# A decoder layer (gated scan, cross-attention, feed-forward) in fp32: first transfers in another order, padded weights fetched in whole rows, and a second table of places for units 0, 1 and 15

## The chip, the cores and the metric

One core of a Trainium2 chip runs the kernel. The metric is the device time of one execution in microseconds (us); host work (laying arrays out) is not in it. The five engines are named as in the profile: PE (TensorE; PEld is its weight load), DVE (VectorE), ACT (ScalarE), POOL (GpSimd) and SP (SyncE, which here only issues transfers). ACT issues transfers too.

## The reference

All in float32, with B = 4 sequences of 1024 tokens, width 256, 16 heads of 16 channels.

```python
# 1. a state-space layer (Mamba-2 form), per head h, state size 64
logA = x_h @ W_logA + b_logA
X, Bm, Cm = split(silu(x_h @ W_XBC + b_XBC))        # 16, 64, 64 channels
cum  = cumsum(logA over time)
Y    = (exp(cum_i - cum_j) for j <= i) * (Cm @ Bm.T) @ X
x    = layernorm(x + ((x_h @ W_gate + b_gate) * Y) @ W_out.T + b_out)
# 2. cross-attention to 77 context tokens per sequence, with a mask
q = x @ q_w + q_b ; k, v = split(ctx @ kv_w + kv_b)
x = layernorm(x + softmax(q k.T / 4, masked) v @ proj_w + proj_b)
# 3. feed-forward, 256 -> 1024 -> 256, ReLU
x = layernorm(x + relu(x @ W1 + b1) @ W2 + b2)
```

## The kernel before

The 4096 tokens are cut into 16 **units** of 256 tokens, four to a sequence; a unit has two chunks of 128. Each unit u passes three stages: A (state-space layer, `stage_a` and `chunk_a`), B (attention, `stage_b`) and C (feed-forward, `stage_c`). The scan over 1024 tokens is done chunk by chunk: inside a chunk by a masked 128x128 matrix per head, between chunks through a 64-wide state.

Every small piece of a stage is a **part** with a name and a place. `WHEN` (L36) gives each name a number, and unit u's part stands at u + WHEN[name]; all parts of all units, and the setup blocks (names with s_), are sorted by that number and emitted in that order (L1069). Each engine runs its instructions in the order in which they were emitted, so the table sets the order of the work on all five engines and on the two transfer queues. A place of -1.9 means: about two units ahead of the unit's own time.

The pieces that the change and the prediction touch:

- `load_u(u)` (L142) fetches xu, the unit's input with the features on the partitions: 256 KB in 256 rows of 1 KB, and the source is walked as `a x k t` with a of size 2 outermost. Two of its readers are pl (L486, the logA projection, on PE) and px (L618).
- `load_t(u)` (L150) fetches the same input in another layout (xt, four transfers of 16 partitions) for pb (L556), the projection to Bm and Cm.
- pl goes to cum (L494, a scan on DVE), cum to DRAM (cd, L501), and from there cd is read back broadcast to all partitions: four transfers dl (L509, 512 KB each, one per chunk c and half k, dl00 to dl11) and ec (L516). The exponentials on ACT (ex, L679), the causal select on POOL (sel, L687) and the product with pg on DVE (st, L711) work on dl in place. de (L651, DVE) reads a corner of dl.
- bct (L576, DVE) with th (L568, ACT) is the silu of pb; pg (L701), ptb (L719), pc (L752), py (L798), pyo (L737), poa (L825) are stage A's other matmuls. pq (L855), pm (L880), pe (L927), pa (L952) and pob (L988) are stage B's, ph (L1018) and pf (L1045) are stage C's. pk (L363) and pv (L394) make the keys and values once.
- The setup blocks fetch constants: s_x (L176) the first xu and xt, w_bc, w_l, b_l; s_g the weights w_x, b_x, w_g on ACT's queue; s_x2 scales w_x and b_x by 0.5 on POOL (L236); s_c the context, the weights of keys and values, k_b and the masks; s_o the gate's bias b_g in eight transfers (L303) and w_out in eight (L310); s_q the queries' weights; s_p, s_1, s_2 the later weights. `packed` (L260) fetches the keys' or queries' weights, which lie padded in DRAM (16 used columns of each 32), in pieces of 16 columns.

Transfers from SP and ACT share eight completion semaphores. A transfer that is given a semaphore again waits, in its queue, until the former transfer with that semaphore has landed; all that stands behind it in that queue waits too.

Of the kernel before, what the change touches and what calls it, by code (L numbers as in the profile page):

```python
# [18 lines left out]
S = 77  # L19
FF = 1024  # L20
P = 128
# [12 lines left out]


WHEN = {  # L36
    "s_c": -11.4319, "s_z": -9.9133, "s_x": -9.8561, "load_u1": -8.0656, "s_g": -6.4870,
    "keys": -5.3615, "s_l": -4.6719, "s_x2": -4.4990, "values1": -4.1376, "s_bc": -3.7603,
    "values3": -3.4250, "load_u": -2.5586, "values2": -1.9971, "pl": -1.8803, "cum": -1.8531,
    "keys0": -1.8267, "px1": -1.7594, "zx1": -1.7162, "px0": -1.5890, "cd": -1.5818,  # L40
    "load_t": -1.5536, "zx0": -1.5509, "pcum": -1.4767, "ncum": -1.4509, "s_p": -1.2104,
    "thx0": -1.1705, "thx1": -1.1208, "dl00": -1.0934, "dl01": -1.0768, "dl10": -0.9492,
    "dl11": -0.9057, "keys1": -0.8509, "s_o": -0.8374, "de0": -0.8294, "pb0": -0.8117,
    "th00": -0.8019, "xz1": -0.7953, "ex00": -0.7869, "bct00": -0.7866, "th01": -0.7453,
    "bct01": -0.6793, "sel00": -0.6211, "xz0": -0.6048, "load_k0": -0.5874, "pb1": -0.5858,
    "ec": -0.5819, "ex01": -0.5770, "sel01": -0.5599, "ptb00": -0.5404, "th10": -0.5257,
    "bct10": -0.5205, "pgt": -0.5199, "bk00": -0.4948, "gT": -0.4894, "dex0": -0.4785,
    "xw0": -0.4447, "th11": -0.4309, "de1": -0.4269, "bct11": -0.4250, "pg00": -0.3724,
    "pg01": -0.3720, "st00": -0.3610, "st01": -0.3602, "ex11": -0.3481, "sel11": -0.3410,
    "ptb01": -0.3408, "bk01": -0.2802, "ex10": -0.2757, "ecx": -0.2676, "pyo0": -0.2315,  # L50
    "pc0": -0.2303, "py0": -0.2272, "pg11": -0.2257, "pg10": -0.2148, "ptb10": -0.1983,
    "load_k": -0.1849, "xb": -0.1554, "ya0": -0.1481, "yg0": -0.1318, "bk10": -0.0982,
    "sn0": -0.0665, "pts0": -0.0616, "sel10": -0.0538, "st11": -0.0434, "dex1": -0.0212,
    "new0": -0.0173, "xw1": -0.0163, "st10": 0.0043, "ptb11": 0.0094, "poa0": 0.0190,
    "s_q": 0.0209, "bk11": 0.0220, "pyo1": 0.0432, "r10": 0.0459, "py1": 0.0504, "mv_a0": 0.0672,
    "rs_a0": 0.1161, "ya1": 0.1433, "pc1": 0.1487, "ln_a0": 0.1570, "sn1": 0.1632, "yg1": 0.1757,
    "poa1": 0.2004, "pts1": 0.2036, "r11": 0.2185, "mv_a1": 0.2296, "values0": 0.2451,
    "new1": 0.2563, "rs_a1": 0.3220, "ln_a1": 0.3476, "pt_b0": 0.4352, "pt_b1": 0.4430,
    "xT_b": 0.4675, "pq": 0.5617, "q": 0.5703, "pm1": 0.7199, "mx1": 0.7334, "pm0": 0.7620,
    "mx0": 0.7696, "pmt": 0.9324, "qm0": 0.9930, "qm1": 0.9996, "pe0": 1.0418, "es00": 1.0464,  # L60
    "s_2": 1.0775, "pe1": 1.0783, "es01": 1.0868, "pa0": 1.1557, "es10": 1.1603, "es11": 1.1757,
    "ot0": 1.1769, "om0": 1.1956, "pa1": 1.2797, "x1b": 1.2868, "ot1": 1.2885, "om1": 1.3653,
    "o1": 1.4120, "o0": 1.4426, "pob0": 1.4994, "pob1": 1.5308, "r20": 1.5433, "mv_b0": 1.5643,
    "r21": 1.5897, "rs_b0": 1.5947, "mv_b1": 1.6135, "rs_b1": 1.6195, "ln_b0": 1.6688,
    "ln_b1": 1.7529, "pt_c1": 1.8663, "pt_c0": 1.9377, "s_1": 2.0149, "xT_c": 2.0215,
    "x2b": 2.0830, "ph0": 2.1982, "ph1": 2.3198, "h0": 2.3291, "h1": 2.3786, "ph2": 2.4035,
    "ph3": 2.4579, "h2": 2.4605, "h3": 2.5019, "pf00": 2.6426, "pf01": 2.7349, "r30": 2.7932,
    "pf10": 2.8269, "mv_c0": 2.9076, "pf11": 3.0362, "r31": 3.0394, "mv_c1": 3.1693,
    "rs_c0": 3.6344, "ln_c0": 3.9014, "rs_c1": 3.9589, "out0": 3.9632, "ln_c1": 4.0359,
    "out1": 5.0081,  # L70
}


# [1 line left out]
def decoder_layer_kernel(ctx: ExitStack, tc: tile.TileContext, a: dict, out: bass.AP):  # L75
# [27 lines left out]

    def part(u, name):
        def put(fn):
            jobs.append((u + WHEN[name], len(jobs), name, fn))

        return put

# [37 lines left out]
        )  # L147
        xus[u] = xu

    def load_t(u):  # L150
        for r in range(4):
            nc.sync.dma_start(
                out=xts[u % 2][32 * r : 32 * r + CH],
                in_=a["xT"][CH * r : CH * r + CH, :, u * T : (u + 1) * T],
            )
# [19 lines left out]

    @setup("s_x")  # L176
    def _():
        load_u(0)
        nc.vector.memset(w_l0, 0.0)
        nc.vector.memset(w_l, 0.0)  # L180
        nc.vector.memset(b_l, 0.0)
        for half in range(2):
            rows_ = slice(64 * half, 64 * half + 64)
            nc.scalar.dma_start(out=w_l0[rows_, half], in_=xgl[0:64, half, :, 128:XW])
        for k in range(2):
            nc.scalar.dma_start(
                out=b_l[32 * k : 32 * k + 8],
                in_=xgl[64:65, :, k, 128:XW].rearrange("o a r -> r a o"),
            )
        nc.vector.memset(xts[0], 1.0)  # L190
        load_t(0)
        nc.vector.memset(w_bc, 0.0)
        for r in range(4):
            own = slice(NS * (r % 2), NS * (r % 2) + NS)
            nc.scalar.dma_start(
                out=w_bc[32 * r : 32 * r + CH],
                in_=a["w_bc"][CH * r : CH * r + CH, :, :, r // 2, own],
            )
        nc.scalar.dma_start(
            out=w_bc[CH::32], in_=a["w_bc"][64].rearrange("g b q (n s) -> (q n) (g b) s", n=2)  # L200
        )
        make_identity(nc, ident)
        nc.gpsimd.tensor_copy(b_l[64:128], b_l[0:64])

# [11 lines left out]

    @setup("s_g")
    def _():
        nc.gpsimd.memset(w_x, 0.0)
        nc.gpsimd.memset(w_g, 0.0)  # L220
        for half in range(2):
            rows_ = slice(64 * half, 64 * half + 64)
            nc.scalar.dma_start(
                out=b_x[:, half], in_=xgl[64, half, :, 0:64].partition_broadcast(P)
            )
            nc.scalar.dma_start(out=w_x[rows_, :, half, :], in_=xgl[0:64, half, :, 0:64])
            for k in range(2):
                nc.scalar.dma_start(
                    out=w_g[rows_, k, :, half, :],
                    in_=xgl[0:64, half, k, 64:128].rearrange("x (r c) -> x r c", c=CH),  # L230
                )
# [25 lines left out]

    ctx_ = {}

    def packed(n, kk):  # L260

        return a[n][kk * P : kk * P + P].rearrange("p g (r c) -> p (g r) c", c=32)[:, :, 0:CH]

    def by_heads(t, n):

# [6 lines left out]
    @setup("s_c")  # L272
    def _():
        kv_w = tile_([P, FF // P, T], "hT", "kv_w", bufs=1)
        ctx_.update(k_w=kv_w[:, 0:2], v_w=kv_w[:, 4:6])
        for n, f in (("valid", 2), ("kc", 6)):
            ctx_[n] = kv_w[:, f : f + 2].rearrange("p f t -> p (f t)")[:, 0 : B * S].rearrange(
                "p (b s) -> p b s", b=B
            )
        ctxT = ctx_["ctxT"] = tile_([P, 2, 2 * T], "qm", "ctxT", bufs=1)  # L280
        v_b = ctx_["v_b"] = tile_([S, D], "on", "v_b", bufs=2)
        nc.sync.dma_start(
            out=ctxT[:, :, 0 : B * S], in_=a["ctxT"].rearrange("(k p) s -> p k s", p=P)
        )
        nc.sync.dma_start(out=ctx_["v_w"], in_=a["v_w"].rearrange("(k p) e -> p k e", p=P))
        for kk in range(2):
            nc.sync.dma_start(
                out=ctx_["k_w"][:, kk].rearrange("p (m c) -> p m c", c=CH), in_=packed("k_w", kk)
            )
        nc.sync.dma_start(out=v_b, in_=a["v_b"].partition_broadcast(S))  # L290
        by_heads(k_b, "k_b")
        nc.sync.dma_start(
            out=mrow.rearrange("p b s -> p (b s)"), in_=a["mask"][0].partition_broadcast(P)
        )
        nc.sync.dma_start(out=mcol, in_=a["maskT"])
        nc.gpsimd.memset(vz, 1.0)

    @setup("s_o")
    def _():
        for half in range(2):  # L300
            for r in range(4):
                at = 32 * r + CH * half
                nc.sync.dma_start(  # L303
                    out=b_g[at : at + CH],
                    in_=xgl[64, half, :, 64 + CH * r : 64 + CH * r + CH].rearrange("k c -> c k"),
                )
        for half in range(2):
            for r in range(4):
                at = 32 * r + CH * half
# [5 lines left out]

    @setup("s_q")
    def _():
        for kk in range(2):
            nc.sync.dma_start(
                out=q_w[:, kk].rearrange("p (m c) -> p m c", c=CH), in_=packed("q_w", kk)  # L320
            )
        by_heads(q_b, "q_b")

    @setup("s_p")
# [825 lines left out]
```

## Time and profile before

| | |
|---|---|
| median of 3 runs | 717.74 us (717.26 to 718.21) |
| the profiled execution | 715.87 us, of which the span from first to last instruction is 714.2 us |
| PE busy | 678.8 us, 95% of the span |
| DVE, ACT, POOL busy | 546.9, 413.9, 275.6 us |
| first matmul that reads xu (L486) | 19.77 us into the span |
| first dl transfer issued (L509) | 30.43 us |
| first matmul of unit 0 for Bm and Cm (L556) | 34.77 us |
| PE in each 100 us between 200 and 600 us | busy 100.00 us |
| TensorE clock granted, mean of the span | 0.972 of full |

The profile is one execution; its times are about 1.9 us under the median of the runs. "Busy" of PE counts a matmul from its start to its modelled end, so a busy PE may still run at half clock; the clock row must be read beside it. A row of the timeline begins with its start and its length, then engine, line and what is written and read, and in brackets the idle time before it and what ended that.

### The profile page before, as it was taken

What the parts mean: (1) busy time and instruction counts of PE and PEld (TensorE: products, weight loads), DVE (VectorE), ACT (ScalarE), POOL (GpSimd) and SP (SyncE); (2) the same over time, 40 slices, a digit from 0 to 9 for tenths busy, and PEclk for the clock granted to TensorE, in tenths of its full rate; (3) what the DMA queues carried; (4) which work ended last, traced back from release to release, by engine and by line L of the source; (5) the groups of instructions that cost most, each with busy time, mean ns of one, the idle gap of its engine ahead of it and who ended that gap; (6) DMA issues with size and microseconds to landing.
All of it is one profiled execution on the core that took longest, in us unless ns stands there. A gap on an engine that the chain in (4) does not pass through costs nothing.

```text
span 714.2 us, 19432 instructions
## 1 busy us (share of the span) xinstructions
PE 678.8 (95%) x7744; PEld 538.8 (75%) x7744; DVE 546.9 (77%) x1337; ACT 413.9 (58%) x1091; POOL 275.6 (39%) x441
## 2 busy tenths in 40 slices
PE   2588999999999999999999999999999999999996
PEld 1256767887878787787878788787878788787785
DVE  2376899878888787888788887888878788877652
ACT  0185787747585665748576474847566474843210
POOL 3133355334433443343433434353434334342241
PEclk8578999999999999999999999999999999999999
DMA  5456755224240423424140422424042332200001
GB/s 89 93 144 144 185 173 165 78 61 122 68 116 18 127 61 96 103 75 123 53 124 24 123 76 75 123 61 128 25 123 62 101 83 75 61 17 1 16 16 37
DMA packets 104566, 61.47 MB, mean 86 GB/s; under 512 B 15695, under 2 KB 102172, under 8 KB 104476
## 3 DMA queue, kind: packets, MB, share of 16 engines
q1 hardware_dynamic: 101632, 59.83, 31.9%
q8 instruction: 61, 1.00, 0.5%
q10 hardware_dynamic: 2844, 0.41, 0.4%
q14 instruction: 29, 0.24, 0.1%
HBM read 54.98 MB, written 5.24 MB: 84 GB/s over the span
## 4 chain that ended last, share of the span: by engine, by line
PE 87%; DMA 6%; ACT 2%; SPq 2%; DVE 1%; issue 1%; POOL 0%; POOLq 0%; ACTq 0%; DVEq 0%
PE pf L1045 16%; PE ph L1018 16%; PE pg L701 8%; PE pb L556 5%; PE pe L927 5%; PE pa L952 4%; PE po_b L988 4%; PE py L798 4%; PE pq L855 4%; PE po_a L825 4%; DMA xu<-in_xT_dram 3%; PE ptb L719 3%; PE pm L880 3%; PE py L737 2%; PE pc L752 2%; PE pgt L585 2%
## 5 line engine op out<-in xcount | busy, mean ns | idle before, releaser
L679 ACT ACTIVATE dl<-dl,ncum 128x128 f32<-128x128 f32 x512 | 156.3, 395 | 1.7 <-DVE de L651 1.7
L1045 PE MATMUL pf<-w,hT 128*128 128x256 f32 x512 | 123.5, 386 | 0.0
L1018 PE MATMUL ph<-T_c,w 128*128 128x256 f32 x512 | 121.0, 385 | 0.0
L1018 PEld LDWEIGHTS ph<-T_c,w 128*128 128x128 f32 x512 | 93.7, 190 | 23.0 <-issue 5.9
L938 ACT ACTIVATE es<-pe,mb 77x512 f32<-77x512 f32 x128 | 76.9, 679 | 52.4 <-PE pe L927 51.3
L1045 PEld LDWEIGHTS pf<-w,hT 128*128 128x128 f32 x512 | 93.8, 190 | 15.5 <-issue 2.4
L687 POOL TENSOR_SCALAR_AFFINE_SELECT dl<-dl 128x1024 f32<-128x1024 f32 x64 | 70.0, 1094 | 48.0 <-ACT dl L679 48.0
L711 DVE TENSOR_TENSOR dl<-pg,dl 128x512 f32<-128x512 f32 x128 | 80.7, 683 | 6.4 <-PE pg L701 5.5
L576 DVE SCALAR_TENSOR_TENSOR bct<-th,pb 128x512 f32<-128x512 f32 x128 | 80.9, 673 | 4.3 <-ACT th L568 4.0
L568 ACT ACTIVATE th<-pb 128x512 f32<-128x512 f32 x128 | 69.1, 594 | 22.4 <-PE pb L556 22.2
L726 ACT COPY bk<-ptb 128x512 f32<-128x512 f32 x56 | 32.8, 585 | 75.8 <-PE ptb L719 75.5
L701 PE MATMUL pg<-bct 64*128 64x128 f32 x1024 | 67.3, 279 | 1.2 <-DVE bct L576 1.0
L701 PEld LDWEIGHTS pg<-bct 64*128 64x128 f32 x1024 | 60.4, 188 | 10.7 <-DVE bct L576 6.0
L891 DVE TENSOR_REDUCE maxes<-pm 128x4 f32<-128x308 f32 x128 | 52.2, 471 | 19.9 <-PE pm L880 19.9
L666 POOL TENSOR_TENSOR xw<-xz,de 128x128 f32<-128x128 f32 x56 | 21.3, 402 | 81.7 <-ACT de L658 80.5
L819 POOL TENSOR_TENSOR yg<-ya,gT 128x256 f32<-128x256 f32 x28 | 21.4, 766 | 68.6 <-DVE ya L812 54.2
L556 PE MATMUL pb<-xt,w_bc 17*64 17x256 f32 x1024 | 44.0, 408 | 2.1 <-DVE bct L576 2.1
L440 POOL TENSOR_SCALAR rs_a<-mv_a 128x1 f32<-128x1 f32 x32 | 7.1, 222 | 94.4 <-DVE mv_a L435 94.4
L1034 ACT ACTIVATE hT<-ph,b 128x256 f32<-128x256 f32 x64 | 26.8, 470 | 27.1 <-PE ph L1018 24.7
L970 POOL TENSOR_TENSOR on<-at,rec 128x256 f32<-128x256 f32 x32 | 21.5, 673 | 54.0 <-DVE rec L965 53.3
L787 ACT COPY state<-pts 64x128 f32<-64x128 f32 x56 | 14.5, 258 | 44.3 <-PE pts L777 44.0
L913 DVE SCALAR_TENSOR_TENSOR qm<-q,own,pmt 128x512 f32<-128x512 f32 x32 | 22.5, 744 | 18.4 <-PE pmt L904 18.4
(122 smaller groups left out, 1247.6 us busy)
## 6 DMA issues: line engine op xcount, KB each, us to landing
dl<-cd SPq DMA_DIRECT2D x64, 512.0 KB
xu<-in_xT_dram SPq DMA_DIRECT2D x16, 256.0 KB
xt<-in_xT_dram SPq DMA_DIRECT2D x64, 64.0 KB
xk<-in_x_dram SPq DMA_DIRECT2D x16, 256.0 KB
ec<-cd SPq DMA_DIRECT2D x16, 256.0 KB
out_dram<-r SPq DMA_DIRECT2D x32, 128.0 KB
w<-in_w_dram SPq DMA_DIRECT2D x2, 1024.0 KB
cd<-cum SPq DMA_DIRECT2D x16, 64.0 KB
```

Of the source, the lines that this page charges most:

```text
L556: nc.tensor.matmul(pbs[r][64 * half : 64 * half + 64, bc, :], lhsT=w_bc[rs, 2 * gk + half, bc, :], rhs=xt[rs, 2 * gk + half, :], start=Tru ...
L568: nc.scalar.activation(th, s[f"pb{gk}"][r], AF.Tanh)
L576: nc.vector.scalar_tensor_tensor(t, s[f"th{gk}{r}"], 1.0, s[f"pb{gk}"][r], ALU.add, ALU.mult)
L679: nc.scalar.activation(dl[:, h, :], dl[:, h, :], AF.Exp, bias=s["ncum"][:, 2 * c + k, h : h + 1],)
L687: nc.gpsimd.affine_select(out=dl, in_=dl, compare_op=ALU.is_ge, fill=0.0, base=0, pattern=[[0, 8], [1, P]], channel_multiplier=-1,)
L701: nc.tensor.matmul(pgs[half][:, r, :], lhsT=t[lo : lo + 64, 0, cs], rhs=t[lo : lo + 64, 1, cs], start=True, stop=True,)
L711: nc.vector.tensor_tensor(d, v[f"pg{k}"][half], d, ALU.mult)
L891: nc.vector.tensor_reduce(mx[:, :, at : at + 2], s[f"pm{c}"][r].rearrange("p k a s -> p a k s"), AX.X, ALU.max, negate=True,)
L927: nc.tensor.matmul(pes[r][:, par, :], lhsT=kT[rs, gp, par, bs], rhs=s["qm"][rs, par, gp, :], start=True, stop=True,)
L938: nc.scalar.activation(e, s[f"pe{gp}"][r], AF.Exp, bias=mb[:, b : b + 1], scale=CH**-0.5)
L1018: nc.tensor.matmul(ph[:, j, :], lhsT=w1[:, k, f * P : (f + 1) * P], rhs=s["xT"][:, k, :], start=(k == 0), stop=(k == 1),)
L1045: nc.tensor.matmul(pf, lhsT=s["hT"][:, f, c * P : (c + 1) * P], rhs=w2[:, f, :], start=(f == 0), stop=(f == FF // P - 1),)
```

## The change

1. In s_x the first transfers are issued in the order xt and w_bc alternating, then xu, then w_l and b_l; before it was xu, w_l, b_l, xt, w_bc. The memsets of w_x and w_g move from s_g to s_x.
2. `packed` fetches the padded rows whole (2 KB runs), into a scratch part of the kv_w tile, and two POOL copies take the used columns out. It serves the keys' and the queries' weights. The tiles `valid` and `kc`, which lay in kv_w, get two buffers of the unitT ring.
3. The eight b_g transfers become a block of their own, s_b, ahead of s_o.
4. All numbers of `WHEN` are new, and `EDGE` gives units 0, 1 and 15 places of their own, which `part` prefers. The setup blocks move in `WHEN`: s_x stands first now, s_c after s_g and s_x2; s_p goes from -1.2 to 1.1, s_q from 0.0 to 0.4, s_2 from 1.1 to 1.7 and s_1 from 2.0 to 1.5.

The order that results on SP's queue is: xt x4, xu(0), cd(0), ctxT, v_w, k_w, v_b, k_b x2, two masks, dl00, dl01, xu(1), ec, b_g x8, dl10, dl11, xk, w_out x8, b_out, cd(1), xk(1), xt(1) x4, dl01(1), ec(1), xu(2), dl00(1), dl10(1), cd(2), q_w, q_b x2, dl11(1). On ACT's queue: w_bc x5, w_l x2, b_l x2, b_x, w_x, w_g x2, b_x, w_x, w_g x2, and then the first computing instruction. PE begins with pl, pb, pgt, pcum, px of unit 0 and no longer with pv.

```diff
 WHEN = {
-    "s_c": -11.4319, "s_z": -9.9133, "s_x": -9.8561, "load_u1": -8.0656, "s_g": -6.4870,
...
-    "load_t": -1.5536, "zx0": -1.5509, "pcum": -1.4767, "ncum": -1.4509, "s_p": -1.2104,
...
+    "s_x": -9.0759, "s_l": -6.2209, "s_g": -6.2074, "s_bc": -5.0504, "s_x2": -4.4536,
+    "s_c": -3.7665, "load_u1": -3.4533, "s_z": -2.9306, "s_b": -2.5309, "load_u": -2.2285,
+    "pl": -1.9502, "cum": -1.9128, "load_k0": -1.9113, "s_o": -1.7308, "px1": -1.7147,
...
+EDGE = {
+    0: {
+        "pl": -4.8683, "pb0": -4.8549, "th00": -4.7365, "pgt": -4.7343, "cum": -4.5273,
...
+        "ec": -3.3456, "de0": -3.2299, "bct11": -3.1934, "ex00": -3.1334, "dex0": -2.9623,
+        "ex01": -2.9401, "xz0": -2.7667, "sel00": -2.6907, "dl10": -2.4731, "ptb01": -2.4202,
...
+    1: {
+        "px0": -3.0462, "zx0": -2.7658, "pl": -2.6367, "cum": -2.4709, "cd": -2.4365,
+        "pcum": -2.3348, "load_k": -2.1146, "load_t": -1.9876, "px1": -1.9399, "zx1": -1.7487,
...
+    15: {
+        "load_u": -4.4549, "load_k": -2.9211, "pl": -2.1881, "cum": -2.0838, "px1": -2.0769,
...
     def part(u, name):
         def put(fn):
-            jobs.append((u + WHEN[name], len(jobs), name, fn))
+            place = EDGE.get(u, {}).get(name, WHEN[name])
+            jobs.append((u + place, len(jobs), name, fn))
...
     @setup("s_x")
     def _():
+        nc.vector.memset(xts[0], 1.0)
+        nc.vector.memset(w_bc, 0.0)
+        for r in range(4):
+            load_t(0, [r])
+            own = slice(NS * (r % 2), NS * (r % 2) + NS)
+            nc.scalar.dma_start(
+                out=w_bc[32 * r : 32 * r + CH],
+                in_=a["w_bc"][CH * r : CH * r + CH, :, :, r // 2, own],
+            )
+        nc.scalar.dma_start(
+            out=w_bc[CH::32], in_=a["w_bc"][64].rearrange("g b q (n s) -> (q n) (g b) s", n=2)
+        )
         load_u(0)
...
-    def packed(n, kk):
-
-        return a[n][kk * P : kk * P + P].rearrange("p g (r c) -> p (g r) c", c=32)[:, :, 0:CH]
+    def packed(t, n):
+        pad = ctx_["kv_w"][:, 0:4].rearrange("p (k f) t -> p k (f t)", k=2)
+        nc.sync.dma_start(out=pad, in_=a[n].rearrange("(k p) g m -> p k (g m)", p=P))
+        for kk in range(2):
+            nc.gpsimd.tensor_copy(
+                t[:, kk].rearrange("p (m c) -> p m c", c=CH),
+                pad[:, kk].rearrange("p (m c) -> p m c", c=32)[:, :, 0:CH],
+            )
...
-    @setup("s_o")
+    @setup("s_b")
     def _():
         for half in range(2):
             for r in range(4):
...
     @setup("s_q")
     def _():
-        for kk in range(2):
-            nc.sync.dma_start(
-                out=q_w[:, kk].rearrange("p (m c) -> p m c", c=CH), in_=packed("q_w", kk)
-            )
+        packed(q_w, "q_w")
         by_heads(q_b, "q_b")
```

## The prediction

> **What bounds the kernel now.** I read first the page's busy times and slices, then the stretches of the span, then the chain that ended last and the timeline around its pieces.
>
> ```profile
> PE 678.8 (95%) x7744; PEld 538.8 (75%) x7744; DVE 546.9 (77%) x1337; ACT 413.9 (58%) x1091; POOL 275.6 (39%) x441
> PE   2588999999999999999999999999999999999996
> PEclk8578999999999999999999999999999999999999
> ```
>
> PE is full from the fourth slice (of 17.9 us) to the last but one. What can be won lies at both ends, or in the order in which PE runs the same matmuls.
>
> ```profile
> 10.00:20.00 10.00, 0.23 (x6) 0.23 (x8) 2.85 (x11) 0.00 (x0) 0.00 (x0) 0.61 0.25 63
> 20.00:30.00 10.00, 3.17 (x14) 1.56 (x7) 4.12 (x12) 1.80 (x2) 1.37 (x2) 0.50 0.42 90
> 40.00:50.00 10.00, 8.99 (x73) 6.17 (x73) 7.11 (x17) 10.00 (x31) 2.94 (x4) 0.68 0.39 98
> 60.00:70.00 10.00, 9.97 (x108) 6.93 (x108) 6.42 (x19) 6.42 (x20) 1.86 (x3) 0.66 0.73 138
> 200.00:300.00 100.00, 100.00 (x1182) 80.00 (x1175) 82.69 (x201) 66.26 (x174) 40.47 (x62) 1.00 0.35 93
> ```
>
> Columns: stretch, its length, PE, PEld, DVE, ACT, POOL busy, granted clock, DMA share, GB/s. Between 10 and 20 us PE waits while the DMA engines are a quarter busy; at 60 to 70 the clock is 0.66. Priced at the pace of the middle (each matmul at its mean start-to-start step between 120 and 640 us), PE's work sums to 659 us. So 55 us are lost: 39 by 60.03 us, 10 more by 110, nothing from there to 660, 1 to 700, and 5 after the last matmul.
>
> ```profile
> 8.17 11.47 DMA xu<-in_xT_dram
> 22.21 8.20 DMA cd<-cum
> 33.66 8.19 DMA dl<-cd
> 48.38 11.52 DMA xu<-in_xT_dram
> ```
>
> The start is a chain of transfers; each row is start and length. xu(0) releases pl at 19.77 us, cd and dl bring the first decay matrices at about 39, and xu(2) ends PE's last long wait:
>
> ```profile
> 60.03 0.66 PE L486 MATMUL pl<-xu,w_l 128*32 128x128 f32 x8 [2.15 <-DMA xu<-in_xT_dram]
> 63.98 0.17 DVE L651 TENSOR_TENSOR de<-dl,ncum 128x8 f32<-128x8 f32 x1 [1.54 <-DMA dl<-cd]
> 74.86 0.17 DVE L651 TENSOR_TENSOR de<-dl,ncum 128x8 f32<-128x8 f32 x1 [1.90 <-DMA dl<-cd]
> 674.95 2.66 PE L952 MATMUL pa<-es,vz 77*32 77x256 f32 x16
> 679.47 1.07 PE L952 MATMUL pa<-es,vz 77*32 77x256 f32 x16
> ```
>
> **The change, part by part: the start.** I follow the new queues.
>
> First, xu(0). The xt memset (0.91 us, from 0.87) releases SP at 1.8; four xt issues at 0.64 each, xu at 4.7. What does xu take? It took 11.5 us twice, and from 14 to 19.6 us, with little but xu moving, the trace gives
>
> ```profile
> DMA packets 336, 0.26 MB, mean 46 GB/s; under 512 B 106, under 2 KB 336, under 8 KB 336
> ```
>
> At 46 GB/s its 256 KB last 5.7 us. The Trainium skill (DMA: Bandwidth & Descriptors, "Why a DMA increments its semaphore by 16 and not by 1") says why: a transfer uses as many engines, up to 16, as divide the slowest dimension of both views, and xu's source has a 2 outermost. Two engines at the page's 27 GiB/s would be an estimated 4.5 us. Three xu transfers stand in the chain below; by the rule's figure the result would be 3.6 us earlier. The row decides. I allow 8.6 us from issue to landing (about 1 to start, 5.7, and 2 for what shares its engines): xu(0) at 13.3, 6.4 us before now.
>
> Next, dl00. ACT's w_g gets xu(0)'s semaphore, so six loads of ACT go out from 13.4 at 0.63 us each, to 17.4. The table load (1.28) and the first tanh stand behind them, 18.7, still ahead of any now. dl00 gets the last w_g's semaphore: landed about 19.3, dl00 issued at 19.7 against 30.43. On SP before it stand cd (after pl and cum, 14.6), ctxT, v_w, k_w, v_b, k_b, masks; at about 0.5 us each they pass by then. dl00 and dl01 land by 27 (four took 8 to 11 us).
>
> Then the lead goes. xu(1) stands behind 1 MB of dl on its two engines: 27 + 6.3 = 33.3, ec 34.7. The seventh and eighth b_g get the semaphores of xu(1) and ec; behind them on SP wait dl10, dl11, xk, w_out and cd(1). dl10 goes at 35.5. The sixth and seventh w_out get the semaphores of dl10 and dl11, which land by 42; then cd(1) at 43.5 (now 47.8), xt(1), dl01(1) at 47 (after cd(1) has landed), ec(1), xu(2) at 48.4: the same as now. And it stands behind 512 KB of dl (4.3 us) and ec (1.4): 48.2 + 5.7 + 6.6 gives 60.5, where pl of unit 2 runs at 60.03 now.
>
> PE has pb of unit 1 done by then (1.2 us of work more), but DVE's cum of unit 2 waits for this pl, and in its queue the residual sum and statistics of chunk 0 (0.42 + 0.43 + 0.18 us) and unit 1's bct stand behind. I count no gain for pb. Gone are the two waits for dl in the rows above: dl01(1) and dl10(1) are issued before 50.5, and dl11(1) at 63 with 4.3 us to land. That is +1.54 + 1.90 - 1.03 - 0.5 = **1.9 us**.
>
> The clock speaks against it: PE has nothing to do from about 49.5 to 60.5. The skill (TensorE: Matmul & The Clock Gate, "What's actually happening") says that an idle window of 3.4 us halves the clock and that a busy one restores it. Now a wait of 2.15 us was followed by 0.66 over ten microseconds: 6.8 us at half. By the rule one window would do, 3.4 us at half, 1.7 us less lost than now; by the row nothing changes. I take the row, and zero.
>
> **Whole rows.** k_w and q_w move 512 KB each in 2 KB runs in place of 256 KB in 64 B pieces. SP saves issue time (k_w 1.82 us, q_w 5.87 in the trace); this is what lets dl11(1) go at 63. Added are two POOL copies each; between the row of a POOL memset of that size (0.31) and of a product (0.77) I take 0.5. POOL is idle then, and keys are wanted only by pk at about 43 us, queries' weights by pq at about 71: cost 0, with a bad cover 1.0 each. The memsets moved behind them on POOL (vz 1.80, xz 0.99, states 0.56, maxes 0.85) end near 26, before xz is needed at 28. valid and kc in their own buffers: 0.
>
> **The middle.** The matmuls are the same. Going from matmuls on part of the array (pb, pg, pm, pa, pe) to whole ones costs a step at the first: a block of eight 256-column matmuls lasts 1.73 us start to start, 1.83 when it comes first; four 128-column transposes 0.436 and 0.492. Now ph, ph, pf, pf, pt, ptb come first in a unit; then poa, pf, pt, ptb, pts, pmt: 2 x (0.10 - 0.06) = 0.09 us less, in 13 units **1.2 us**. The tightest new waits are pmt after the second maxes (3.9 us of PE work between, about 1.6 us of DVE) and the first pe after qm: both hold.
>
> **The end.** In unit 15 pa comes straight behind pe and waits for the exponentials: 2.66 us against 1.07. Now a ph block (1.83 us) goes between: **1.5 us**, less than the difference, since ACT's first four exponentials need 2.4.
>
> Sum: 1.9 + 1.2 + 1.5 = 4.6. Span 714.2 - 4.6 = 709.6, its execution 711.3; the runs stand 1.87 above the profiled execution, so the median should be **713.1**.
>
> **Rivals.** (1) *The lead is kept.* If transfers behind dl overlap better than I have it (DMA share 0.25 to 0.4 leaves room), xu(2) lands up to 6.4 us earlier and pl of unit 2 with it: 706.7. Against it stand the semaphores handed on to b_g and w_out. (2) *It makes no difference.* The old waits for dl become waits for bct behind the late cum, end and middle give 1 us instead of 2.7: 716.7. (3) *Slower.* Place: SP between dl11 and cd(1). If dl10 and dl11 need the row's 8.19 us each one behind the other, cd(1) goes at 49.5 and xu(2) lands at 66.5, six later: 719.1. It decides from xu(2) at 65.1 on; each microsecond after that is a microsecond over the time before.
>
> **How the numbers follow.** About 0.2% (1.4 us) is what a measurement can tell. My forecast 0.45 (its own range 710 to 715.5), the lead kept 0.30, no difference 0.12, slower 0.13. Faster is the first two with the edges of the fourth left out: 0.75; same 0.13; slower 0.12. The range leaves out the best tenth of (1) and the worst half of (3): 705.5 to 718.8.
>
> **What would show it.** pl of unit 0 near 13.3 and dl00's issue near 19.7; SP standing on b_g for xu(1) and ec until about 35; PE idle for some 10 us before pl of unit 2 at about 60.5; no wait for dl at unit 1's de; PE unbroken in the middle with units 0.1 us shorter; pa of unit 15 without its wait. Wrong it is if xu(2) lands more than 3 us from there, or if the middle shows waits.

## The result, and the profile after

The changed kernel takes 716.78 us (median of 22 runs, 715.49 to 718.74); the kernel before, run beside it, 717.12 us (22 runs). The ratio is 0.9998, with a 95% interval from 0.9988 to 1.0008: no difference that can be measured. The forecast was 713.1 us and a clear gain; the time lies in its range, and the gain did not come.

The page of the changed kernel, and the five stretches that the forecast shows of the kernel before, with 50 to 60 us added:

```profile
PE 677.9 (95%) x7744; PEld 533.2 (74%) x7744; DVE 552.3 (77%) x1337; ACT 411.5 (57%) x1091; POOL 278.8 (39%) x445
PE   1676999999999999999999999999999999999997
PEclk9997999999999999999999999999999999999999
```

```profile
10.00:20.00 10.00, 2.59 (x40) 1.10 (x40) 1.13 (x4) 1.59 (x2) 0.18 (x1) 1.00 0.28 64
20.00:30.00 10.00, 6.74 (x53) 4.50 (x55) 3.75 (x8) 3.06 (x6) 7.30 (x14) 1.00 0.70 193
40.00:50.00 10.00, 8.64 (x80) 5.33 (x79) 5.48 (x21) 6.17 (x20) 0.00 (x0) 0.86 0.61 160
50.00:60.00 10.00, 5.99 (x65) 4.00 (x63) 9.57 (x20) 2.40 (x6) 4.34 (x5) 0.83 0.55 152
60.00:70.00 10.00, 6.81 (x69) 4.66 (x64) 5.89 (x20) 3.52 (x8) 0.72 (x1) 0.67 0.50 138
200.00:300.00 100.00, 100.00 (x1208) 79.03 (x1207) 83.28 (x204) 63.85 (x168) 43.39 (x68) 1.00 0.34 89
```

Unit 0 begins earlier: its pl runs at 14.33 us in place of 19.77, and PE has 2.59 us of work between 10 and 20 us, against 0.23. PE as a whole begins later, since the kernel before ran pv from 5.47 us on. The clock column reads 1.00 up to 30 us, but PE did not run at full pace there: pb's 32 matmuls take 2.01 us at 26.64 and 1.12 at 95.24 (rows below), and this trace holds no record of the clock before 32.7 us. Between 50 and 60 us PE has 5.99 us of work while DVE is busy for 9.57, and in 60 to 70 us PE has 6.81 against 9.97. The middle is full in both. The chain of waits shows the transfers of the start, and the timeline shows, among others, the two places (56.99 and 66.97) where PE stood still late in the start:

```profile
17.74 6.58 DMA w_g<-in_w_xgl_dram
25.97 12.47 DMA ec<-cd
39.29 8.01 DMA dl<-cd
54.88 12.05 DMA xu<-in_xT_dram
```

```profile
14.33 0.65 PE L588 MATMUL pl<-xu,w_l 128*32 128x128 f32 x8 [14.33 <-DMA xu<-in_xT_dram]
22.94 1.19 PE L687 MATMUL pgt<-xu,w_g 128*128 128x256 f32 x2 [6.01 <-POOL w_x L334]
26.64 2.01 PE L658 MATMUL pb<-xt,w_bc 17*64 17x256 f32 x32
56.99 1.08 PE L839 MATMUL py<-bct,state 128*32 128x128 f32 x16 [4.01 <-DVE ncum L635]
66.97 0.66 PE L588 MATMUL pl<-xu,w_l 128*32 128x128 f32 x8 [3.19 <-DMA xu<-in_xT_dram]
95.24 1.12 PE L658 MATMUL pb<-xt,w_bc 17*64 17x256 f32 x32
676.79 1.97 PE L1029 MATMUL pe<-qm,kT 32*77 32x256 f32 x32
678.71 1.99 PE L1120 MATMUL ph<-T_c,w 128*128 128x256 f32 x8
680.63 1.07 PE L1054 MATMUL pa<-es,vz 77*32 77x256 f32 x16
```

The last three rows are the end: a block of ph stands between pe and pa, and pa takes 1.07 us without a wait, where it took 2.66.

For the balance I count lost time as in the forecast, and price every kernel's matmuls at the pace that the kernel before has between 120 and 640 us. The columns are microseconds since the start of the span; the number is how much of them was not PE's work at that pace (one execution each; the last column is taken at the start of the last matmul).

| lost by | 20 | 50 | 70 | 140 | 640 | end |
|---|---|---|---|---|---|---|
| before | 17.2 | 36.3 | 43.1 | 49.0 | 49.1 | 49.5 |
| changed | 18.6 | 33.5 | 45.9 | 53.9 | 52.8 | 51.9 |

From 140 us to the end the changed kernel gains 2.0 us and the one before loses 0.5: middle and end together bring 2.5 us, and 2.7 were forecast. The start loses 4.9 us more, where 1.9 less was forecast. The two executions are 716.5 and 714.2 us of span, 2.3 apart, while the medians are 0.3 apart the other way: some 2.7 us of the difference belong to these two executions. If middle and end gain as much in the others, the medians leave about 2.2 us of loss for the start.

Most of the 2.7 can be seen in the trace. Between 100 and 110 us the changed kernel's granted clock is 0.83, where the kernel before has 1.00, and pob takes 3.65 us. In wout_late, an experiment below with the same matmuls at this place, it takes 1.99:

```profile
104.36 3.65 PE L1090 MATMUL po_b<-p_w,o 128*128 128x256 f32 x8 [0.47 <-DVE o L1080]
104.47 1.99 PE L1093 MATMUL po_b<-p_w,o 128*128 128x256 f32 x8 [0.46 <-DVE o L1083]
```

So 1.7 us of the 4.9 are a fall of the clock in this one execution, and what brought it about is not shown.

### The profile page after: what moved, and what is told of

Its sections match the earlier page's. It is cut to its first block, busy times and chain, and to the rows that moved or that the text cites. A ratio compares the mean times of both kernels' runs of the same rounds, so it can differ in the third digit from the quotient of the medians.

```text
span 716.5 us, 19532 instructions
## 1 busy us (share of the span) xinstructions
PE 677.9 (95%) x7744; PEld 533.2 (74%) x7744; DVE 552.3 (77%) x1337; ACT 411.5 (57%) x1091; POOL 278.8 (39%) x445
## 4 chain that ended last, share of the span: by engine, by line
PE 86%; DMA 8%; DVE 3%; SPq 1%; ACTq 1%; ACT 1%; issue 0%; POOLq 0%; POOL 0%; DVEq 0%
PE pf L1147 16%; PE ph L1120 16%; PE pg L803 8%; PE pe L1029 4%; PE pb L658 4%; PE po_b L1090 4%; PE pa L1054 4%; PE pq L957 4%; PE po_a L927 4%; PE py L900 4%; PE pm L982 3%; PE ptb L821 3%; DMA dl<-cd 2%; PE py L839 2%; PE pc L854 2%; DMA ec<-cd 2%
## 5 line engine op out<-in xcount | busy, mean ns | idle before, releaser
L1147 PE MATMUL pf<-w,hT 128*128 128x256 f32 x512 | 121.2, 382 | 0.0
L1040 ACT ACTIVATE es<-pe,mb 77x512 f32<-77x512 f32 x128 | 77.1, 681 | 40.4 <-PE pe L1029 39.4
L542 POOL TENSOR_SCALAR rs_a<-mv_a 128x1 f32<-128x1 f32 x32 | 8.9, 278 | 117.8 <-DVE mv_a L537 117.6
L658 PE MATMUL pb<-xt,w_bc 17*64 17x256 f32 x1024 | 42.0, 411 | 0.0
L927 PE MATMUL po_a<-w_out,yg 128*128 128x256 f32 x128 | 36.7, 411 | 0.0
L821 PE MATMUL ptb<-ident,bct 128*128 128x128 f32 x224 | 35.0, 280 | 0.2 <-DVE bct L678 0.2
L1029 PE MATMUL pe<-qm,kT 32*77 32x256 f32 x512 | 35.1, 389 | 0.0
```

Of the source, the lines that this page charges most:

```text
L658: nc.tensor.matmul(pbs[r][64 * half : 64 * half + 64, bc, :], lhsT=w_bc[rs, 2 * gk + half, bc, :], rhs=xt[rs, 2 * gk + half, :], start=Tru ...
L927: nc.tensor.matmul(v["po"], lhsT=v["yg"][:, k, :], rhs=w_out[:, k, :], start=(k == 0), stop=(k == 1),)
L1029: nc.tensor.matmul(pes[r][:, par, :], lhsT=kT[rs, gp, par, bs], rhs=s["qm"][rs, par, gp, :], start=True, stop=True,)
L1040: nc.scalar.activation(e, s[f"pe{gp}"][r], AF.Exp, bias=mb[:, b : b + 1], scale=CH**-0.5)
L1147: nc.tensor.matmul(pf, lhsT=s["hT"][:, f, c * P : (c + 1) * P], rhs=w2[:, f, :], start=(f == 0), stop=(f == FF // P - 1),)
```

## The experiments

Every ratio is to the kernel before, run on the same chip beside it; places in the diffs are those of the two tables.

**The middle and the end alone.** `MID` and `EDGE` are the changed kernel's places.

```diff
-            jobs.append((u + WHEN[name], len(jobs), name, fn))
+            place = WHEN[name]
+            if 3 <= u <= 14 and name in MID:
+                place = MID[name]
+            place = EDGE.get(u, {}).get(name, place)   # EDGE holds 15 only
+            jobs.append((u + place, len(jobs), name, fn))
```

> The kernel before, with the new places for the parts of units 3 to 14 and for unit 15 only; the first transfers, the setup blocks and units 0 to 2 as before. Theory (the start loses what middle and end gain): the first 60 us stay as before (pl of unit 2 at about 60.0), the middle saves 0.09 us in each of 12 or 13 units (1.2 in all; between the two traces PE's work fell by 1.5) and the end 1.5: ratio to before about 0.996, 714.1 to 714.6. Rival (the new order of the middle and the end is worth nothing, and the start was neutral): ratio 1.000, 717.1.

Measured: 717.64 us, ratio 1.0013 (1.0004 to 1.0023). Not the theory. Lost time stays with the kernel before up to 60 us (39.4), goes on to 51.4 by 140 and 55.0 by 260, and only then falls, to 53.9 at 640 and 53.1 at the last matmul. Before 140 us PE has a wait of 2.84 us (at 77.27, for bct) and then 3.4 us at half clock. Between 140 and 260 us it has neither and is busy all the time, but its matmuls follow each other more slowly: the 96 of pe take 1.7 us more there than as many between 280 and 400, those of pf 1.2 more and those of pa 0.7. So changing over from one order to the other in mid-run cost PE 3.6 us in this stretch; this kernel doesn't give the price of the middle alone. The gain after the changeover, 1.1 us from 260 to 640, is as large as that of the changed kernel from 140 to 640.

**What the start waits for: xu(2), or the keys.** In the changed kernel DVE's queue has the keys' vector work (kT, means, km, L472 to L487) ahead of unit 1's ncum, which holds PE at 56.99 for 4.01 us; then xu(2) holds it at 66.97 for 3.19.

```profile
50.62 0.79 DVE L472 TENSOR_SCALAR kT<-T_b_kc,own,held 128x308 f32<-128x308 f32 x2 [0.26 <-ACT T_b_kc L470]
54.62 2.21 DVE L487 TENSOR_SCALAR km<-T_b_kc,own 128x308 f32<-128x308 f32 x2
56.76 0.18 DVE L635 TENSOR_SCALAR ncum<-pcum 128x32 f32<-128x32 f32 x1
```

Some 2.3 us of this delay is work that takes longer here than it did: km 2.21 us in place of 0.87 in the kernel before (row below, with the keys and values), and the step ahead of it (L483) 1.93 in place of 0.93, while POOL runs xb and two selects from 53.11 to 56.66 us. In the second kernel below (keys_early), where the same work runs on DVE while POOL has none, km takes 0.67. That POOL is the cause is not tested.

Three kernels move the one, the other, and both:

```diff
 EDGE = {
+    2: {"load_u": -4.36},                          # u2_early, u2_keys
-    "keys": -0.8695, ... "keys0": -0.5265,
+    "keys": -1.33, ... "keys0": -1.32,             # keys_early, u2_keys
```

> The changed kernel with one transfer moved: xu of unit 2 goes straight behind dl11 of unit 0 on SP (about 39.9 us) in place of 54.9; nothing else changes its place. Theory (PE waits for xu(2) as in rival 3, but the keys' vector work on DVE, 48.5 to 56.8, keeps PE busy late too): xu(2) lands near 53, the wait of 3.19 us before pl(2) goes, and pl(2) runs at about 63.8: 3.2 us less than the changed kernel, about 713.5. If xu(2) alone is the cause of the lost time: pl(2) at 60.5 or before, 5 to 6 us less, about 711. If xu(2) is not the cause (the dl transfers behind it, the clock): under 1 us.

> The changed kernel with the first half of the keys (pk on PE and its vector work on DVE, 8 us) placed ahead of unit 0's second decay corner (de1), where DVE waits for dl10 and dl11 from 41 to 47, and not behind it, ahead of unit 1's ncum. xu(2) stays at 54.9. Theory (two locks in a row): ncum of unit 1 at 49 to 50 in place of 56.8, PE's wait of 4.01 us at 57 goes, but pl(2) still waits for xu(2) at 66.97: within 1 us of the changed kernel. If the keys alone are the cause: 4 us less.

> Both moves in the changed kernel: xu(2) straight behind dl11 and the first half of the keys ahead of de1. Theory (two locks in a row, each hiding the other): pl(2) at 59 to 60.5 in place of 66.97, and the changed kernel's time less 6 to 7 us, about 710; more than the sum of the two alone (3.2 and 0 to 1). Rival (the moves act alone, and the rest is lost to the clock and to dl of units 1 and 2): no more than 4 us less, 713 or above.

Measured: 718.19 us (1.0026, 1.0016 to 1.0036), 717.57 us (1.0012, 1.0005 to 1.0019) and 718.84 us (1.0032, 1.0019 to 1.0044). None is faster than the changed kernel, and only the second came about as the theory had it (by the ratios it is 1.0 us slower). There the wait for ncum is gone, and the wait for xu(2) has taken it over:

```profile
67.09 0.65 PE L588 MATMUL pl<-xu,w_l 128*32 128x128 f32 x8 [6.72 <-DMA xu<-in_xT_dram]
```

With xu(2) early, pl(2) has no wait, and runs later than ever, at 67.85. SP and PE of that kernel:

```profile
40.96 0.53 SPq L243 DMA_DIRECT2D xu<-in_xT_dram  x1
41.54 6.20 SPq L258 DMA_DIRECT2D xk<-in_x_dram  x1
...
55.34 0.56 SPq L604 DMA_DIRECT2D cd<-cum  x1
```

```profile
61.58 3.03 PE L659 MATMUL pb<-xt,w_bc 17*64 17x256 f32 x32 [5.83 <-DMA xt<-in_xT_dram]
```

The issue of the small xk behind dl10, dl11 and xu takes 6.20 us (1.91 in the changed kernel, where no xu stands there). So SP is late with w_out, cd(1) goes at 55.3 and not at 49.8, and PE waits for xt in place of xu. In the kernel with both moves cd(1) is as late (55.62), and PE waits 5.83 us, until 62.03, for the product of pg with dl. Neither xu(2) nor the keys is the one cause: behind each lock stands the next.

**The places named by the failed steps.** One kernel moves w_out behind xt(1), out of the way of cd(1) (the place of rival 3). The other moves the context's 1.1 MB behind ec, out of the way of w_g and dl00 (the first step of the forecast that was off).

```diff
-"s_o": -1.7308   # w_out                    (wout_late; the row b_out goes with load_k0)
+"s_o": -0.98
+"s_d": -3.34     # ctxT, v_w, k_w, v_b, k_b, masks; in s_c before (ctx_late)
+"s_e": -1.0      # POOL's two copies of k_w
```

> The changed kernel with the eight w_out transfers moved on SP from ahead of cd(1) to behind xt(1); the row b_out stays ahead of cd(1). Theory (cd(1) and xt(1) stand behind w_out, which waits for dl10 and dl11 to land: the place of rival 3): cd(1) at 42 to 43 in place of 49.76, xt(1) by 46, dl01(1) at about 49.5 in place of 53.6, xu(2) at about 51 in place of 54.9, pl of unit 2 at about 63; 2 to 4 us less than the changed kernel. Rival (the keys' vector work ahead of unit 1's ncum holds PE anyway, or what follows unit 2 eats it): under 1 us.

> The changed kernel (one transfer for each xu) with the context's transfers (ctxT, the weights of keys and values, v_b, k_b, the masks) moved on SP from between cd(0) and dl00 to behind ec of unit 0; the two POOL copies of the keys' weights go to a later place. Theory (the step that failed first: w_g stands behind these 1.1 MB on the DMA engines, lands at 24.3 and not at 19.3, and hands its semaphore to dl00): dl00 issued at 19.5 to 20.5 in place of 24.34, pgt of unit 0 at 19 to 20 in place of 22.9; the later steps earlier by 2 to 4 us, the time 1 to 3 us less than the changed kernel. Rival (SP's queue is full from then on whatever the order): dl00 early, but dl10, cd(1) and xu(2) where they are (38.8, 49.8, 54.9), the time within 1 us.

Measured: 717.73 us (1.0016, 1.0007 to 1.0026) and 718.37 us (1.0023, 1.0012 to 1.0034). Each moved its transfer as meant, and xu(2) hardly at all; SP, and then POOL, with the context behind ec:

```profile
18.45 1.14 SPq L626 DMA_DIRECT2D dl<-cd  x2
...
39.65 1.05 SPq L626 DMA_DIRECT2D dl<-cd  x2
...
49.78 0.56 SPq L618 DMA_DIRECT2D cd<-cum  x1
...
54.89 0.57 SPq L242 DMA_DIRECT2D xu<-in_xT_dram  x1
```

```profile
52.54 1.26 POOL L537 TENSOR_TENSOR xb<-xk,row_b_out 128x512 f32<-128x512 f32 x1 [14.74 <-DMA row_b_out<-in_b_out_dram]
53.74 0.74 POOL L371 COPY kv_w<-kv_w 128x256 f32<-128x256 f32 x2
```

dl00 is 5.9 us earlier; dl10, cd(1) and xu(2) stand within a microsecond of where they stood (38.81, 49.76, 54.88). pk now waits 4.58 us for the copies of k_w, and this wait the edit itself has made: at their new place the copies stand on POOL behind xb, which waits 14.74 us for the row b_out. So this kernel doesn't give the price of the context's place alone. With w_out moved, cd(1) goes at 43.01 in place of 49.76, but w_out still waits for dl11 and dl01(1) stands behind it: xu(2) goes at 54.61, and pl(2) runs at 66.16. The rival of the first expectation holds: no gain. That of the second holds for the transfers, but by the ratios the time is 1.8 us above the changed kernel's, and not within 1.

**The slow transfer.** xu in two halves, in both kernels:

```diff
-        nc.sync.dma_start(out=xu, in_=a["xT"][0:64, ...].rearrange("x (k a) t -> a x k t", a=2))
+        for half in range(2):
+            nc.sync.dma_start(
+                out=xu[64 * half : 64 * half + 64],
+                in_=a["xT"][0:64, ...].rearrange("x (k a) t -> a x k t", a=2)[half])
```

> The changed kernel with each xu fetched as two transfers, one for each half of the partitions, whose outermost size is 64 and not 2. Theory (an xu of one transfer moves on two DMA engines at 46 GB/s, holds what shares them, and keeps SP's queue full, which is where the issue of ec, 5.0 us, and of dl behind xu(2), 5.1, went): pl of unit 0 from 14.3 to below 12, the issue of ec below 2 us, dl10 of unit 0 at 35 or before in place of 38.8, cd of unit 1 at 46 or before in place of 49.8, pl of unit 2 below 63; 3 to 6 us less than the changed kernel. Rival (the two halves bring nothing, since dl fills all engines, and cost 0.6 us of SP's time a unit): within 1 us.

> The same on the kernel before. Theory: xu(0), 11.5 us from issue to landing, in under 5; pl of unit 0 at 14 to 16 in place of 19.77, and the whole start with it, 3 us or more less than before. If less than 1 us comes out, another transfer (w_x, w_g on ACT's queue, xt) holds the start right behind xu.

> Both: xu in two halves, w_out behind xt(1). Theory: the gains add in part, pl of unit 2 at about 58 to 60 in place of 66.97, 5 to 8 us less than the changed kernel, 709 to 712. If neither alone nor both move the time by more than 1 us, SP's transfers are not what the start waits for, and the order of the engines' own work in units 0 to 3 is.

Measured: the changed kernel 707.56 us (0.9884, 0.9868 to 0.9899), the kernel before 705.19 us (0.9848, 0.9834 to 0.9863), the changed kernel with w_out moved as well 706.14 us (0.9861, 0.9842 to 0.9880). This is the largest gain found, 8 us on the changed kernel and 11 on the kernel before by the ratios, where the theories had 3 to 8. The second is the fastest kernel of all, and the changed order is slower on top of it: 2.6 us by the ratios. First the changed kernel with halves, then the kernel before with halves:

```profile
9.92 0.65 PE L589 MATMUL pl<-xu,w_l 128*32 128x128 f32 x8 [9.92 <-DVE w_l L309]
57.58 0.65 PE L589 MATMUL pl<-xu,w_l 128*32 128x128 f32 x8
```

```profile
12.93 0.65 PE L487 MATMUL pl<-xu,w_l 128*32 128x128 f32 x8 [3.02 <-DMA xu<-in_xT_dram]
48.60 0.40 PE L487 MATMUL pl<-xu,w_l 128*32 128x128 f32 x8
```

In the kernel before xu(0) now goes at 8.21 and releases pl at 12.93, 4.7 us after its issue and not 11.5. Between 10.4 and 11.4 us the DMA engines are busy all the time and move 307 GB/s (xt and b_x are among it); with xu in one transfer they were busy for 0.15 of the time from 14 to 19.6 us, at 46 GB/s. In the changed kernel pl of unit 2 has no wait any more; yet it runs 9 us later than in the other, so xu(2) is not what sets the two apart.

**The keys and values.** In the kernel before, 12 of the 16 pv and all 8 pk matmuls (4.7 us at 0.22 to 0.26 each) and the 29 vector instructions (9.8 us) ran between 5 and 39 us, while PE and DVE waited for the first transfers. PE and DVE of the kernel before, with their idle time in brackets:

```profile
5.47 4.45 PE L394 MATMUL pv<-kv_w,ctxT 128*77 128x256 f32 x12 [5.47 <-DMA kv_w<-in_v_w_dram]
25.86 0.79 DVE L370 TENSOR_SCALAR kT<-kv_w,own,held 128x308 f32<-128x308 f32 x2 [4.88 <-ACT kv_w L368]
28.86 0.87 DVE L385 TENSOR_SCALAR km<-kv_w,own 128x308 f32<-128x308 f32 x2
```

In the changed kernel this work stands between 39 and 63 us, and DVE's part takes 12.1 us. The first kernel here moves that work alone, with every transfer of the kernel before in its order; the second does it with the halves.

```diff
-"keys": -5.3615, "keys0": -1.8267, "keys1": -0.8509,
-"values1": -4.1376, "values3": -3.4250, "values2": -1.9971, "values0": 0.2451,
+"keys": -0.8695, "keys0": -0.5265, "keys1": -0.1473,
+"values2": -1.6828, "values3": -1.4022, "values0": -0.9822, "values1": 0.3684,
```

> The kernel before, all transfers in its order; only the work of keys and values (16 pv and 8 pk matmuls on PE, 29 instructions of 9.8 us on DVE) gets the places that it has in the changed kernel, so that it runs among units 0 and 1 in place of 5 to 39 us. Theory (that move costs the start what the changed kernel lost): 3 to 5 us more than before, 720 to 722, with PE's lost time at 140 us at 52 to 54 in place of 49. Rival (PE waits for transfers until 60 us anyway and the work hides there): within 1 us.

> The kernel before with xu in halves (705.2), and only the work of keys and values at its later places. Theory (that work is what the changed order of the start pays): 5 to 8 us more, 710 to 713, as it was 7.5 us without the halves; lost time at 140 us 43 to 46 in place of 38.3. Rival (with the halves PE has room in units 0 and 1): within 2 us.

Measured: 723.86 us (1.0104, 1.0082 to 1.0125), 7.5 us slower, and 712.85 us (0.9945, 0.9929 to 0.9961) against 705.19, 7.7 us by the medians and 6.9 by the ratios. The direction is that of both theories; the first had the price too low (3 to 5 us), the second has it in its range. It is the largest single price found in the change. PE of the first:

```profile
28.31 1.22 PE L618 MATMUL px<-w_x,xu 128*128 128x128 f32 x4 [8.68 <-POOL w_x L236]
65.19 0.66 PE L777 MATMUL pts<-ident,stateT 128*128 128x128 f32 x2 [4.75 <-DVE stateT L763]
```

Up to 28 us the transfers come within about two microseconds of before, but PE's waiting time is empty (2.6 us of pv are missing in it by 20 us); and at 65 PE waits for a state that stands behind the keys on DVE. Lost time by 140 us is 57.0 in place of 49.0, and with the halves 46.0 in place of 38.3. The price is PE standing still: by 140 us it is busy for 102.3 us in place of 110.0, and with the halves for 111.7 in place of 119.2.

Putting that work back into the changed kernel was tried in three ways: the first half of the keys behind the last product of pg with dl; the context's transfers behind ec, with halves; and the transfers straight behind xu(0), with the work straight behind unit 0's cum and ncum.

```diff
+"keys0": -0.23                                             # halves_keys
+"s_d": -3.34, "s_e": -1.0                                  # halves_ctx
+"s_d": -7.5, "s_e": -4.40, "values0..3": -4.526 to -4.523,  # ctx_first, halves_ctx_first
+"keys": -4.522, "keys0": -4.20, "keys1": -3.60, "pgt" of unit 0: -4.50
+"s_o": -0.98                                               # and halves_ctx_wout
```

> The changed kernel with xu in halves (707.6), and the first half of the keys' vector work on DVE (kT, the means, km: 44.4 to 50.5 there) moved from ahead of unit 1's ncum to behind the last product of pg with dl of unit 0. Theory (PE's wait of 4.14 us for ncum at 50.75 is what the changed order of the keys costs): ncum of unit 1 at 44 to 45, that wait gone, pl of unit 2 at about 54 in place of 57.6, 3 to 4 us less than with the halves alone, 703.5 to 704.5. Rival (other work of units 1 and 2 is late anyway): less than 1 us.

> The changed kernel with xu in halves (707.6), and the context's transfers behind ec of unit 0. Theory (w_g behind the context's 1.1 MB holds pgt of unit 0 and dl00): pgt at 14 to 15 in place of 18.6, dl00 at 15 to 16 in place of 19.8; 2 to 4 us less than with the halves alone. Rival (cd(0), its landing and the later transfers set the start): dl00 1 us earlier at most, the time within 1 us.

> The changed kernel, one transfer for each xu; the context's transfers go on SP straight behind xu(0), where SP stands idle from 5.5 to 15.5 us, and the work of keys and values straight behind unit 0's cum and ncum, where PE stands idle from 17 to 23. Theory: pv and pk done by 27, DVE's keys by 32, lost time at 140 us at 48 to 50 in place of 53.9, the time 3 to 5 us less than the changed kernel, 712 to 714. Rival (the two slow engines of xu(0) get an eighth of 1.1 MB more, xu(0) lands 3 us later, and PE then waits for xu(2) as before): within 1 us, or slower.

> The same with xu in halves (707.6 without the move). Theory: 3 to 5 us less, 702.5 to 704.5, below the kernel before with the halves (705.2) since the new middle and end come on top. Rival (as above): 707 or more.

> The same, and w_out behind xt(1) (which took 1.4 us off with the halves alone). Theory: 701 to 703.5, the fastest of all. Rival: no further gain, since cd(1) isn't what waits once DVE is free: within 0.7 us of the run without it.

Measured, in that order: 708.36 us (0.9879, 0.9860 to 0.9899), 710.12 (0.9908, 0.9890 to 0.9926), 719.95 (1.0048, 1.0028 to 1.0068), 715.14 (0.9988, 0.9976 to 0.9999), 717.01 (1.0007, 0.9996 to 1.0018). No theory held; in the first the rival did (the time is that of the halves alone). In the first the wait for ncum is gone and one of 3.02 us for ACT's copy of pk has come, at 55.06. In the second dl00 goes at 14.03, and pk waits 5.38 us for POOL's copies of k_w, which stand behind xb as in ctx_late; so it too doesn't give the price of the place. In the last three the keys stand in the way of unit 0 itself: its bct comes late behind them, PE stands 1.9 to 3.3 us at a time between 24 and 44 us, and pl of unit 1 runs at 46.56 (with halves) in place of 36.48. The kernel before had the keys' work in a stretch in which neither unit 0 nor unit 1 had anything to do. In these three ways I found no such place in the changed one.

**Middle and end once more, and the whole rows alone.** The first is midtail's edit and the halves; the second takes from the change this and nothing else (k_w in s_c and q_w in s_q, and buffers of their own for valid and kc):

```diff
-    def packed(n, kk):        # two transfers each, 16 of every 32 columns
+    def packed(t, n):         # one transfer of whole rows, then two POOL copies
```

> The kernel before with xu in halves (705.2), and the new places for the parts of units 3 to 14 and of unit 15. Theory (the new middle is worth 1.1 us and the new end 1.9 once the ramp is over, but going over to the new order costs 4 to 6 us of PE in units 2 to 5, as it did without the halves): 705.5 to 708, not faster than the kernel before with the halves. Rival (middle and end come free where the start isn't late): 702 to 703.

> The kernel before with the whole rows alone: k_w and q_w in one transfer of 512 KB each in place of two of 128 KB in pieces of 64 B, two POOL copies for each, the masks' rows in buffers of their own. Theory (forecast: cost 0): within 1 us of before. Rival (512 KB ahead of xu(0) hold it up, or the copies hold POOL ahead of w_x): 1 to 3 us slower; or the 7 us of issue time that SP saves bring 1 to 2 us.

Measured: 705.69 us (0.9850, 0.9827 to 0.9873), the same as the kernel before with halves, as the theory had it: 37.8 lost by 140 us, 41.2 by 260, 40.3 by 640. And the whole rows in the kernel before: 721.07 us (1.0050, 1.0033 to 1.0067), 3.6 us slower, against a forecast of nothing. Up to 60 us the two are alike (39.4 lost); then, on POOL and PE:

```profile
66.09 0.74 POOL L266 COPY q_w<-kv_w 128x256 f32<-128x256 f32 x2 [9.73 <-DMA kv_w<-in_q_w_dram]
66.92 0.23 POOL L441 TENSOR_SCALAR rs_a<-mv_a 128x1 f32<-128x1 f32 x1
67.23 0.57 POOL L442 TENSOR_TENSOR rs_a<-rs_a,mhalf 128x1 f32<-128x1 f32 x1
67.77 0.72 POOL L820 TENSOR_TENSOR yg<-ya,gT 128x256 f32<-128x256 f32 x1
```

```profile
68.55 2.08 PE L826 MATMUL po_a<-w_out,yg 128*128 128x256 f32 x4 [5.72 <-POOL yg L820]
```

The copies take 0.74 us, but they stand in POOL's queue until q_w has landed, with unit 0's yg behind them. In the changed kernel they run at 73.88, 5.1 us after q_w's issue, and no wait for q_w is shown.

## Why the prediction was wrong

**What held.** The end: pa of unit 15 without its wait, 2.66 to 1.07 us; 1.3 us by the lost time after 640 us (0.9 gained, where the kernel before loses 0.4), 1.5 forecast. The middle: 1.2 us between 140 and 640 (1.1 gained against 0.1 lost), as forecast, and no waits in it. The lead at the start: pl(0) at 14.33 against 13.3. The semaphores: b_g's seventh and eighth issue waited for xu(1) and ec, until 38.5, and w_out's seventh for dl11, until 47.3. The waits for dl at unit 1's de are gone. From 40 to 70 us the clock cost nothing more: 0.86, 0.83 and 0.67 in the three stretches, against 0.68, 1.00 and 0.66. The 1.7 us behind 104.3 us come on top in the profiled execution.

**The first step that failed** is "dl00 gets the last w_g's semaphore: landed about 19.3". w_g landed 6.58 us after 17.74, together with the context's transfers, which I let pass on SP and did not price on the DMA engines: dl00 at 24.34 and not at 19.7. With the context behind ec it went at 18.45. Two more terms follow: dl10 and dl11 took 8.5 us and not 6.5, and what SP had to issue behind them 2.5 and not 1.5. So cd(1) went at 49.76 (43.5), xu(2) at 54.88 (48.4), pl(2) at 66.97 (60.5): the place and nearly the number of rival 3, which had xu(2) land at 66.5. The start came out about 2.2 us slower by the medians where 1.9 us of gain was forecast. But rival 3's price, a microsecond for each that xu(2) is late, is not shown: the kernel with dl00 early, the one with cd(1) early and the one with xu(2) early were none of them faster.

**The largest price has no term in the sum.** The forecast prices transfers, the four copies and the new order of middle and end. The work of the keys and values itself, 20 matmuls and 29 vector instructions that the change takes out of the first 39 us, is put at nothing without a reason. "keys are wanted only by pk at about 43 us, queries' weights by pq at about 71: cost 0" is said of the copies; I asked when the keys are wanted, and not what their work had stood on. And "PE has nothing to do from about 49.5 to 60.5" leaves that work out: between 50 and 60 us PE had 5.99 us of work, and DVE 9.57. It had filled time in which PE and DVE waited, and moved it stands in units 0 and 1. That move alone costs the kernel before 7.5 us. In the changed kernel lost time is 2.8 us less than before at 50 us, and 4.9 more at 140, of which 1.7 are the clock. How much of the rest is this work, and how much is SP's late transfers, no run separates, since in the changed kernel each move met the next lock. With the halves, where neither kernel waits for xu(2), the difference by 140 us is 4.7 (43.0 against 38.3), in two executions within 0.2 us of their medians. That the moved work decides in the changed kernel too is argued, not shown.

**Whole rows** had the bad cover priced at 1.0 us each; in the kernel before it is 3.6. What counts is not the copy, but what is behind it in POOL's queue while it waits.

**Rival 2** named the time, 716.7, by luck and not for the reason: the waits that took over were for ncum and xu(2), and middle and end gave 2.5 us and not 1. The forecast's range holds the time by luck as well: a gain of 2.5 and a loss of about 2.2 cancel.

**Small slips.** PE's row of the kernel before is a 9 from the fifth slice on, not from the fourth. The sum for pl of unit 2 starts at 48.2, where the text has xu(2) at 48.4. Neither changes the result.

**The row and the rule.** The row (46 GB/s) was right for the xu that both kernels have. The rule that I set beside it (the Trainium skill, DMA: Bandwidth & Descriptors, "Why a DMA increments its semaphore by 16 and not by 1"), that the slowest dimension decides how many engines a transfer uses, agrees with the experiment: with 64 outermost in place of 2 the same 256 KB land in 4.7 us, not 11.5. The forecast took from the page only what two engines could bring, 3.6 us; what another shape would bring, 8 and 11 us, it did not ask.

## What to carry to other kernels

Work that fills a wait can be free where it stands and dear elsewhere: before moving it, list what each engine runs during the wait and price all of it at the new place, on every engine's queue. In this start the next lock stood close behind the first, so no single edit of the order brought anything, and the transfer that is slow by its shape was worth more than the order of all. A small instruction that waits for a transfer costs what stands behind it in its queue; two of my own edits showed that once more.

## What the runs showed of the hardware that I had not expected

Issuing a transfer can itself take microseconds, with no semaphore wait shown. Behind two dl (512 KB each) and one xu in one transfer, the next issue took 5.00 us in the changed kernel; with xu in halves that same issue took 0.63 (the two halves of xu took 2.92 together):

```profile
25.38 0.54 SPq L242 DMA_DIRECT2D xu<-in_xT_dram  x1
25.97 5.00 SPq L618 DMA_DIRECT2D ec<-cd  x1
```

```profile
20.86 2.92 SPq L243 DMA_DIRECT2D xu<-in_xT_dram  x2
23.82 0.63 SPq L619 DMA_DIRECT2D ec<-cd  x1
```

After two dl alone it took 1.91 us (xk), after two dl and an xu 6.20. It looks as if a queue holds only so much that has not landed; this is argued from these numbers, and no run was made for it.
